# Issuing the product dt*u and the first two softmax minima one tick later

## The chip, the cores and the metric

The kernel runs on one core of a Trainium2 chip. The metric is device microseconds for one execution, as the median of several runs. A core has five engines that work side by side, each through its own queue in order: TensorE (PE, matmuls), VectorE (DVE), ScalarE (ACT), GpSimd (POOL) and SyncE (SP), which here issues all DMAs.

## The reference, cut to what matters

Two layers work on 4 images of 384 channels and 32 x 32 pixels, all in float32.

- Layer 0 is a selective scan over the 1024 pixels in four directions: groupnorm, a projection to dt, B and C, then for each of 384 channels and 16 states

```
dt = softplus(W_dt (W_x u) + bias)
h  = h * exp(dt * A) + (dt * u) * B
y  = sum over states of h * C
```

  followed by a sum over directions, a layernorm over channels, GELU and the residual.
- Layer 1 works on the 1024 pixels as tokens: layernorm, attention with one head of 384, residual; layernorm, four experts of 384 to 1536 to 384 with GELU, mixed by a top-2 gate (all four are computed densely), residual.

The reference's causal mask, softmax and gate are all computed.

## The kernel before, in words

**Units and ticks.** The scan is cut into 768 units: 4 images x 3 channel blocks of 128 x 2 pairs of directions x 2 directions x 4 groups of 4 states x 4 groups of 32 channels. A unit's tile is 128 x 1024 (32 channels x 4 states on the partitions, pixels along the row). A loop written out by hand (lines 1287 to 1315) issues one unit per turn, called a tick: `decay` puts exp(dt A) for unit t + 2 on ACT (L550), `front` the product v = du * B on DVE (L557), `back` the product h * C of unit t - 1 on POOL (L570), held until v of this tick is done, `middle` the scan on DVE (L563), and `row`, every fourth tick, the matmuls that sum over states into y (L595). While image 0 is scanned, v of many units comes from PE instead: `feed` scales a transposed du on ACT (L798, tiles st), and `turned` transposes it back on PE (L815).

**What runs between.** All other work is written as Python generators that the loop advances a little in each tick. `yield "wait", n` stops one for n ticks, `yield "pe", x` takes x us off a budget of PE work per tick (4.4 in attention, 3.3 in experts). `defer(n, f)` calls f at the beginning of the tick n later, `defer(n, f, inner)` in that tick between v and the scan. The order within a tick is: decay; deferred calls; v; the product on POOL; the `inner` calls; the scan; `row`; the fetches of dt, du, B and C for units 3 to 5 ticks ahead; one step of the next image's preparation; then side work and, with what is left of the budget, attention and experts of the image whose scan is done. So the scan of image b runs beside the preparation of image b + 1 and the attention and experts of image b - 1. After tick 768 only the last image's attention and experts are left.

**Projection (L407 to L445).** `preparation(b)` calls `project_dt` for each channel block m and pair, twelve ticks apart from b = 1 on. In tick s it takes its tiles and issues the matmuls of the first half (L423); in s + 1 softplus of that half on ACT (L429) and the matmuls of the second; in s + 2 its softplus; in s + 3 the store of dt for the first direction (L435) and the product dt*u on DVE (L437); in s + 4 the store of that du (L439), the store of dt and the product of the second direction; in s + 5 the last store. The loads of later units read dt and du back from DRAM.

**Slots.** Eight tiles of SBUF, the slots, are shared by projection, experts' weights (w, up to four chunks ahead, L1102 to L1109), layernorm's squares (three), attention's tiles, residual tiles (xe, xr) and `feed`. `take` waits for a free one; a slot given back rests one tick and goes to the end of the line. Four PSUM banks (two while image 0 is scanned) are shared in the same way.

**Attention (L843 to L995).** `scores(i)` issues the score matmuls of the 128 tokens of block i (L897, and the mask's L902), one or two PSUM banks of up to 512; `softmax(i)` takes the row's minimum on DVE (L911; scores carry a minus sign), exp with its sum on ACT (L915), and gives the banks back; one tick later the row is normalised. Block i is transposed for the value product when the scores of block i + 3 are due, one block per tick.

Of the kernel before, what the change touches and what calls it, by code (L numbers as in the profile page):

```python
# [15 lines left out]
P = 128  # L16
# [4 lines left out]
L = HW * HW  # L21
# [28 lines left out]
def hybrid_kernel(  # L50
# [63 lines left out]
    inner = {}  # L114

    def defer(ticks, f, where=due):
        where.setdefault(clock[0] + ticks, []).append(f)

    class Shared:
# [31 lines left out]
    slots = Shared(  # L151
        SLOTS, lambda i, name, *shape: slotp.tile(list(shape), F32, tag=f"s{i}", name=name), 1
    )
# [139 lines left out]
    def columns(v):  # L293

        return v.rearrange("p (h w) -> p w h", w=HW)
# [111 lines left out]
    def project_dt(b, pair, m, u, xd):  # L407

        ks = PAIRS[pair]
        while not slots.ready(3 + pair):  # L410
            yield "wait", 1
        v = u[m]
        if pair == 1:
            v = slots.now(f"ut_{b}_{m}", P, L)
            nc.scalar.copy(v.rearrange("p (w h) -> p w h", h=HW), columns(u[m]))
        dts = [slots.now(f"dt_{b}_{k}_{m}", P, L) for k in ks]
        for h in range(NH):
            while not banks.ready(2):
                yield "wait", 1
            pss = [banks.now(f"pdt_{b}_{k}_{m}_{h}") for k in ks]  # L420
            for i, k in enumerate(ks):
                r = slice(64 * pair + 32 * i, 64 * pair + 32 * i + R)
                nc.tensor.matmul(  # L423
                    pss[i], wdt[r, m * P : (m + 1) * P], xd[r, bass.ts(h, 512)],
                    start=True, stop=True,
                )
            yield "wait", 1
            for i, k in enumerate(ks):
                nc.scalar.activation(  # L429
                    dts[i][:, bass.ts(h, 512)], pss[i], AF.Softplus, bias=dtb[:, k, m : m + 1]  # L430
                )
                banks.give(f"pdt_{b}_{k}_{m}_{h}")
        yield "wait", 1
        for i, k in enumerate(ks):
            nc.sync.dma_start(dts_d[b, k][0, m * P : (m + 1) * P, :], dts[i])  # L435
            du = yield from slots.take(f"du_{b}_{k}_{m}", P, L)
            nc.vector.tensor_mul(du, dts[i], v)  # L437
            yield "wait", 1
            nc.sync.dma_start(dts_d[b, k][1, m * P : (m + 1) * P, :], du)  # L439
            if b == 0:  # L440
                stored_du.add((k, m))
            slots.give(f"dt_{b}_{k}_{m}", f"du_{b}_{k}_{m}")
        if pair == 1:
            slots.give(f"ut_{b}_{m}")
# [34 lines left out]
    def preparation(b):  # L479

        u = first_x if b == 0 else load_image(b)
        yield "wait", 3
        yield from groupnorm(b, u)
        while clock[0] < IMAGE * (b - 1) + 24:

            yield "wait", 1
        xd = one.tile([P, L], F32, tag="xd", name=f"xd_{b}")
        if b == 0:
            nc.scalar.activation(dump, eps, AF.Softplus)
            scan_weights()  # L490
        yield from project_x(b, 0, u, xd)
        if b == 0:
            fetch(-3, ("bc",))
            first_dt(u, xd)
            yield "start", 0
        yield from project_x(b, 1, u, xd)
        for m in range(M):
            for pair in range(2):
                if b > 0 or m > 0 or pair > 0:
                    yield from project_dt(b, pair, m, u, xd)  # L500
                yield "wait", 0 if b == 0 and m == 0 else 12
# [341 lines left out]
    def attention(b, yb, fx0):  # L843
# [47 lines left out]
        def scores(i):  # L891
            ss = []
            for o in range(0, (i + 1) * P, 512):
                e = min((i + 1) * P, o + 512)
                ps = yield from banks.take(f"ss_{b}_{i}_{o}")
                for c in range(M):
                    nc.tensor.matmul(  # L897
                        ps[:, : e - o], qt[:, c, i * P : (i + 1) * P], xn[:, c, o:e],
                        start=(c == 0), stop=(c == M - 1 and e <= i * P),
                    )  # L900
                if e > i * P:
                    nc.tensor.matmul(ps[:, e - o - P : e - o], ident, causal, start=False, stop=True)  # L902
                ss.append((o, e, ps[:, : e - o]))
                yield "pe", 2.6 * (e - o) / 512
            pr = prs[i] = yield from slots.take(f"pr_{b}_{i}", P, L)
            defer(1, lambda: softmax(i, ss, pr), inner)

        def softmax(i, ss, pr):
            nb = sm.tile([P, 4], F32, tag="nb", name=f"nb_{b}_{i}")
            for n, (o, e, ps) in enumerate(ss):  # L910
                nc.vector.tensor_reduce(nb[:, n : n + 1], ps, AX.X, ALU.min)  # L911
            if len(ss) == 2:
                nc.vector.tensor_tensor(nb[:, 0:1], nb[:, 0:1], nb[:, 1:2], ALU.min)
            for n, (o, e, ps) in enumerate(ss):
                nc.scalar.activation(  # L915
                    pr[:, o:e], ps, AF.Exp, bias=nb[:, 0:1], scale=-1.0,
                    accum_out=nb[:, 2 + n : 3 + n],
                )
                banks.give(f"ss_{b}_{i}_{o}")
            defer(1, lambda: normalise(i, nb, len(ss)))  # L920

        def normalise(i, nb, n):
            wd = (i + 1) * P
            if n == 2:
                nc.vector.tensor_add(nb[:, 2:3], nb[:, 2:3], nb[:, 3:4])
            nc.vector.reciprocal(nb[:, 2:3], nb[:, 2:3])
            nc.scalar.activation(prs[i][:, :wd], prs[i][:, :wd], AF.Copy, scale=nb[:, 2:3])
# [62 lines left out]
        for n in range(NB + 3):  # L990
            if n >= 3:
                yield from turn(n - 3)
            if n < NB:
                yield from scores(n)
            yield "wait", 1  # L995
            if n >= 3 and n % 2 == 0:
                yield from values((n - 3) // 2)
# [372 lines left out]
```

## Time and profile before

| | |
|---|---|
| Median of 5 runs | 3821.51 us (3819.53 to 3822.94) |
| The profiled execution | 3824.38 us |
| Its span | 3822.6 us |
| Busy in the span: PE, DVE, ACT, POOL | 89%, 78%, 55%, 48% |
| Mean granted PE clock | 0.915 |
| Scan of a unit on DVE, 768 times | 2284 ns each |
| Product v on DVE, 688 times | 1242 ns each |
| Product dt*u on DVE, 46 times | 1491 ns (ut) and 1401 ns (x) each |
| Product h * C on POOL, 768 times | 2367 ns each |

The scans begin at 47.7 us; image 0's scan lasts until some 714 us, and the last scan starts at some 3147 us. From there on the last image's attention and experts keep PE busy to the end. A row of the groups or the timeline has: source line, engine, operation, result <- inputs with their tiles' names, shape, count, busy time, mean; and in the timeline, in brackets, how long the engine stood still before it and for whom. The view of waits adds these idle times up by pairs: who waited, for whom, microseconds in total, times, the longest. The chain is followed back from the last instruction: at each step to what released it.

### The profile page before, as it was taken

How to read it: one execution, taken by the hardware profiler on the slowest of the kernel's cores; microseconds unless marked ns; L12 is line 12 of the kernel's file. 1: busy time of each engine (PE TensorE's matmuls, PEld its weight loads, DVE VectorE, ACT ScalarE, POOL GpSimd, SP SyncE). 2: the span in 40 equal slices, each digit the busy share in tenths (PEclk: the TensorE clock that was granted, in tenths of full speed). 3: DMA queues.
4: the chain of work that ended last, by engine and by line, in shares of the span. 5: the costliest groups of instructions: out<-in, count | busy, mean ns of one | idle time of the engine just before them, and what ended most of it. 6: DMA issues, size and time to landing. Idle time of an engine off the chain costs nothing.

```text
span 3822.6 us, 33900 instructions
## 1 busy us (share of the span) xinstructions
PE 3383.2 (89%) x11367; PEld 1502.9 (39%) x11367; DVE 2990.5 (78%) x2094; ACT 2104.6 (55%) x2695; POOL 1816.6 (48%) x776
## 2 busy tenths in 40 slices
PE   4666665689999999799999999789999999999999
PEld 1123332235334334345333343354343434644444
DVE  6999899998899999989988999999999992210000
ACT  4688988555666656556565555455555552422121
POOL 2677677644455555545555565455566560000000
PEclk7676677689999999999999999899999999999999
DMA  6564555445576666535756656345566551222321
GB/s 209 206 221 180 214 201 212 182 155 186 182 245 224 220 241 224 178 120 204 240 190 229 215 195 208 136 151 205 198 208 232 190 180 38 89 74 84 94 84 52
DMA packets 407838, 678.26 MB, mean 177 GB/s; under 512 B 33472, under 2 KB 280560, under 8 KB 407664
## 3 DMA queue, kind: packets, MB, share of 16 engines
q1 hardware_dynamic: 401456, 675.70, 51.6%
q8 instruction: 90, 1.47, 0.2%
q10 hardware_dynamic: 6208, 0.39, 0.1%
q14 instruction: 84, 0.69, 0.1%
HBM read 604.04 MB, written 71.96 MB: 177 GB/s over the span
## 4 chain that ended last, share of the span: by engine, by line
PE 42%; DVE 38%; ACT 10%; issue 7%; DMA 2%; POOL 1%; SPq 0%; DVEq 0%; POOLq 0%; ACTq 0%
DVE h L563 22%; PE ph L1154 15%; PE fy L1179 14%; DVE v L557 11%; PE y L595 3%; ACT da L550 3%; ACT st L798 2%; PE pq L868 2%; PE pv L879 2%; PE ss L897 2%; DVE fy L1188 1%; PE po L963 1%; PE pxd L392 1%; ACT L550 1%; ACT L429 1%
## 5 line engine op out<-in xcount | busy, mean ns | idle before, releaser
L570 POOL TENSOR_TENSOR h<-h,bc 128x1024 f32<-128x1024 f32 x768 | 1815.5, 2367 | 1334.8 <-DVE v L557 1147.1
L563 DVE TENSOR_TENSOR_SCAN h<-da,v 128x1024 f32<-128x1024 f32 x768 | 1751.5, 2284 | 109.5 <-PE v L815 18.5
L550 ACT ACTIVATE da<-dt,a 128x1024 f32<-128x1024 f32 x768 | 875.9, 1146 | 937.4 <-DVE h L563 890.3
L1154 PE MATMUL ph<-fx,w 128*128 128x512 f32 x2304 | 1022.6, 600 | 7.0 <-ACT dt L429 3.0
L1179 PE MATMUL fy<-ht,w 128*128 128x512 f32 x2304 | 1022.5, 601 | 1.0 <-ACT dt L429 0.9
L557 DVE TENSOR_TENSOR v<-du,bc 128x1024 f32<-128x1024 f32 x688 | 854.2, 1242 | 34.9 <-DMA du<-dts 14.8
L1154 PEld LDWEIGHTS ph<-fx,w 128*128 128x128 f32 x2304 | 434.4, 191 | 583.2 <-issue 531.0
L1179 PEld LDWEIGHTS fy<-ht,w 128*128 128x128 f32 x2304 | 436.9, 192 | 576.0 <-issue 551.6
L595 PE MATMUL y<-h,sel 128*32 128x512 f32 x3072 | 533.5, 676 | 140.5 <-POOL h L570 140.4
L1139 ACT ACTIVATE ht<-ph,b1s 128x512 f32<-128x512 f32 x384 | 257.5, 678 | 459.2 <-PE ph L1154 458.4
L1188 DVE SCALAR_TENSOR_TENSOR fy<-fy,b2s,tw 128x512 f32<-128x512 f32 x96 | 72.2, 752 | 426.0 <-PE fy L1179 426.0
L595 PEld LDWEIGHTS y<-h,sel 128*32 128x32 f32 x3072 | 101.4, 116 | 478.5 <-POOL h L570 248.4
L815 PE MATMUL v<-ident,st 128*128 128x128 f32 x640 | 134.2, 381 | 98.5 <-DVE h L563 96.9
L798 ACT ACTIVATE st<-dut,bt 128x128 f32<-128x128 f32 x640 | 205.0, 501 | 0.1
L1143 ACT ACTIVATE ht<-ht 128x3072 f32<-128x3072 f32 x64 | 176.8, 2763 | 0.8
L815 PEld LDWEIGHTS v<-ident,st 128*128 128x128 f32 x640 | 109.2, 199 | 161.1 <-issue 87.8
L550 ACT ACT_TABLE_LOAD x110 | 141.1, 1283 | 14.1 <-DMA dt<-dts 11.0
L423 PE MATMUL pdt<-xd,wdt 12*128 12x512 f32 x184 | 84.0, 805 | 65.6 <-ACT dt L429 34.2
L963 PE MATMUL po<-pt,vt 128*128 128x256 f32 x480 | 105.3, 368 | 7.3 <-ACT pt L859 7.3
L897 PE MATMUL ss<-axn,qt 128*128 128x512 f32 (+3 forms) x288 | 105.2, 512 | 3.1 <-ACT pr L915 2.7
L963 PEld LDWEIGHTS po<-pt,vt 128*128 128x128 f32 x480 | 93.1, 195 | 22.6 <-ACT pt L859 9.5
L911 DVE TENSOR_REDUCE nb<-ss 128x1 f32<-128x512 f32 (+3 forms) x48 | 26.0, 553 | 79.0 <-PE ss L902 63.7
(201 smaller groups left out, 1653.5 us busy)
## 6 DMA issues: line engine op xcount, KB each, us to landing
bc<-rows SPq DMA_DIRECT2D x384, 512.0 KB, 4.8
w<-in_w SPq DMA_DIRECT2D x384, 384.0 KB, 6.1
dt<-dts SPq DMA_DIRECT2D x192, 512.0 KB, 4.2
du<-dts SPq DMA_DIRECT2D x192, 512.0 KB, 6.7
dts<-dt SPq DMA_DIRECT2D x48, 512.0 KB, 3.6
dts<-du SPq DMA_DIRECT2D x48, 512.0 KB, 3.5
fx<-t2d SPq DMA_DIRECT2D x12, 768.0 KB, 6.0
tw<-mkd SPq DMA_DIRECT2D x32, 256.0 KB, 6.7
```

The lines of the kernel that those rows point to most:

```text
L550: nc.scalar.activation(u["da"], spread["dt4", n], AF.Exp, scale=a4[:, g, u["q"] : u["q"] + 1])
L557: return nc.vector.tensor_tensor(u["v"], spread["du4", n], spread["bc", n][:, 0, :], ALU.mult)
L563: nc.vector.tensor_tensor_scan(u["h"][:, ::step], u["da"][:, ::step], u["v"][:, ::step], 0.0, op0=ALU.mult, op1=ALU.add,)
L570: product = nc.gpsimd.tensor_tensor(h, h, spread["bc", n][:, 1, :], ALU.mult)
L595: nc.tensor.matmul(y, sel, h, start=first, stop=last, tile_position=(0, jj * DJ))
L798: nc.scalar.activation(st[:, t, :].rearrange("p (d i) -> p i d", i=NI)[:, i, :], dut[:, t, :], AF.Copy, scale=bt[:, u["pair"], t, u["i"] * ...
L815: nc.tensor.transpose(u["v"][:, t * P : (t + 1) * P], st[:, t, u["j"] * P : (u["j"] + 1) * P], ident)
L897: nc.tensor.matmul(ps[:, : e - o], qt[:, c, i * P : (i + 1) * P], xn[:, c, o:e], start=(c == 0), stop=(c == M - 1 and e <= i * P),)
L963: nc.tensor.matmul(pv[:, o:], vt[:, j, m * P : (m + 1) * P], pts[step][j // 4][:, j % 4, o:], start=False, stop=(j == nj - 1),)
L1139: nc.scalar.activation(ht[:, f, :], ps, AF.Identity, bias=bias)
L1154: nc.tensor.matmul(ps, tiles[n][:, c, (f % 2) * P : (f % 2 + 1) * P], xns[h][:, c, :], start=(c == 0), stop=(c == M - 1),)
L1179: nc.tensor.matmul(pss[m], tiles[n][:, f, :], hts[fh][:, f, :], start=(fh == 0 and f == 0), stop=(fh == 1 and f == FH - 1),)
```

## The change

In `project_dt` the two du tiles are taken together with the dt tiles at the start, so that 4 slots (pair 0) or 5 (pair 1) have to be free then, instead of 3 or 4. Both stores of dt are issued in tick s + 3. For images 1 to 3 there is then one tick more before the first product, so that the products come in s + 4 and s + 5, the stores of du in s + 5 and s + 6, and the slots are given back a tick later; for image 0 the products stay in s + 3 and s + 4. In attention, the softmax of blocks 0 and 1 is called two ticks after their scores instead of one; blocks 2 to 7 keep one.

```diff
     def project_dt(b, pair, m, u, xd):
 
         ks = PAIRS[pair]
-        while not slots.ready(3 + pair):
+        while not slots.ready(4 + pair):
             yield "wait", 1
...
-        dts = [slots.now(f"dt_{b}_{k}_{m}", P, L) for k in ks]
+        dts, dus = ([slots.now(f"{x}_{b}_{k}_{m}", P, L) for k in ks] for x in ("dt", "du"))
...
         yield "wait", 1
         for i, k in enumerate(ks):
             nc.sync.dma_start(dts_d[b, k][0, m * P : (m + 1) * P, :], dts[i])
-            du = yield from slots.take(f"du_{b}_{k}_{m}", P, L)
+        if b > 0:
+
+            yield "wait", 1
+        for i, k in enumerate(ks):
+            du = dus[i]
             nc.vector.tensor_mul(du, dts[i], v)
             yield "wait", 1
             nc.sync.dma_start(dts_d[b, k][1, m * P : (m + 1) * P, :], du)
...
             pr = prs[i] = yield from slots.take(f"pr_{b}_{i}", P, L)
-            defer(1, lambda: softmax(i, ss, pr), inner)
+            defer(2 if i < 2 else 1, lambda: softmax(i, ss, pr), inner)
```

## The prediction

> **What bounds the kernel now.** I read the profile in this order: the busy shares, the busy time by windows, VectorE's (DVE's) waits, the chain of waits, and then the rows around each wait that the change can touch. One tick of the schedule is one unit: a product v (1.24 us) and a scan (2.28 us) on DVE; where nothing else is in the way, scans start 3.69 us apart.
>
> ```profile
> PE 3383.2 (89%) x11367; PEld 1502.9 (39%) x11367; DVE 2990.5 (78%) x2094; ACT 2104.6 (55%) x2695; POOL 1816.6 (48%) x776
> ...
> 800.00:1000.00 200.00, 185.95 (x763) 99.86 (x764) 173.04 (x148) 122.80 (x171) 98.04 (x42) 0.95 0.49 168
> 1000.00:1600.00 600.00, 578.84 (x1821) 233.24 (x1820) 570.60 (x386) 365.20 (x352) 344.07 (x146) 0.98 0.64 220
> ...
> 1800.00:2400.00 600.00, 584.65 (x1810) 234.59 (x1808) 561.99 (x368) 347.83 (x332) 345.06 (x147) 0.98 0.62 208
> 2400.00:2600.00 200.00, 167.78 (x710) 90.90 (x711) 186.55 (x148) 93.76 (x132) 99.57 (x43) 0.91 0.46 163
> 2600.00:3148.00 548.00, 543.04 (x1679) 220.06 (x1678) 526.52 (x343) 294.69 (x283) 328.03 (x140) 0.99 0.59 201
> ...
> PE 42%; DVE 38%; ACT 10%; issue 7%; DMA 2%; POOL 1%; SPq 0%; DVEq 0%; POOLq 0%; ACTq 0%
> ```
>
> In a windows row the second number is TensorE (PE) busy, the fourth DVE, the fifth ScalarE (ACT). While experts run (1000 to 1600, 1800 to 2400, 2600 to 3148), PE is busy 96 to 99% and DVE 94 to 96%: two engines sit at the limit together, and the chain changes between them. A DVE wait there is worth no more than what PE can follow. Before 800 us there are no experts and the chain runs over DVE and ACT; after 3148 us it is PE alone. The waits in question:
>
> ```profile
> DVE nb L911 <- PE ss L902: 63.7, 16, 30.5
> ...
> DVE du L437 <- PE ph L1154: 13.0, 2, 8.7
> DVE du L437 <- PE fy L1179: 11.1, 4, 6.1
> ...
> DVE du L437 <- ACT dt L429: 7.0, 9, 2.0
> ...
> DVE du L437 <- DMA dts<-du: 1.2, 1, 1.2
> ...
> 837.06 0.29 DVE L911 TENSOR_REDUCE nb<-ss 128x1 f32<-128x128 f32 x1 [5.34 <-PE ss L902]
> ...
> 1668.08 0.29 DVE L911 TENSOR_REDUCE nb<-ss 128x1 f32<-128x128 f32 x1 [10.76 <-PE ss L902]
> ...
> 2490.74 0.29 DVE L911 TENSOR_REDUCE nb<-ss 128x1 f32<-128x128 f32 x1 [6.16 <-PE ss L902]
> ```
>
> Columns: total, times, longest; then start, duration, and in brackets the idle before. The minimum of the first score block of images 0, 1, 2 holds DVE for 5.34, 10.76 and 6.16 us; the 30.5 us is image 3's, where DVE has no scans left and the wait is free. The product dt*u loses 32.3 us in all, of which 27.9 lie in images 1 and 2 beside attention and experts. One projection while image 0 is scanned shows a second loss:
>
> ```profile
> 509.88 3.06 DVE L437 TENSOR_TENSOR du<-dt,ut 128x1024 f32<-128x1024 f32 x1 [0.53 <-ACT dt L429]
> ...
> 515.06 1.19 DVE L437 TENSOR_TENSOR du<-dt,ut 128x1024 f32<-128x1024 f32 x1
> ...
> 509.49 2.36 POOL L570 TENSOR_TENSOR h<-h,bc 128x1024 f32<-128x1024 f32 x1 [1.00 <-DVE h L563]
> ```
>
> The product came 0.53 us late for softplus; meanwhile GpSimd (POOL) started its own product, and the DVE instruction shows 3.06 us instead of 1.19. The second of the pair did not wait and took 1.19.
>
> **The change, part by part.** No operation is added or removed: 46 DVE products, 96 DMA stores and the minima keep their number and size, so all of it is position.
>
> *A. Image 1's six projections, beside image 0.* Three first products (509.88, 566.45, 624.45) lose 0.53 + 0.50 + 0.52 in waits and (3.06 + 3.04 + 3.02) - 3 x 1.20 = 5.52 in length: 7.1 us. A tick later softplus is long done, the product goes straight behind its scan, and this goes. Each projection now lasts a tick longer, so starts move from ticks 111, 128, 145, 162, 179, 196 to 111, 129, 147, 165, 183, 201 (counted from the waits in the code), and their softplus against ACT's feed copies in other ticks: two scans that waited 3.67 and 3.13 us for PE transposes stuck behind a projection matmul may be spared or another may get this (plus or minus 4). But the chain in those stretches is largely ACT (copies st, softplus, table loads), so some of the 7.1 is found waiting for ACT. I take -5; ends -11 and +2. Next late there: ACT's decays. Image 0's own five projections keep their product's tick and count nothing.
>
> By the Trainium skill (SBUF - State Buffer, section Who interferes with whom), a DVE instruction with two SBUF inputs and a GpSimd one exclude each other, and issue order decides who blocks; the 3.06 beside 1.19 agrees. The rule speaks against the change: were the moved product always second, it would lose up to one POOL product, 2.37 us, twelve times, and part A would be +28 - 7, not -5.
>
> *B. The end of image 1's projection.* The last one ends at tick 207 instead of 201 and holds five of eight slots while attention of image 0 asks for four at tick 206. Three slots have just been used by the x tiles, the third rests until 207, so by my count attention starts one tick late: +3.7 at most once. Experts of image 0 end at tick 393, attention of image 1 starts at 398 with its image, so that most of the shift is taken up there. I take +2; ends 0 and +7.4 (two ticks).
>
> *C. Softmax 0 and 1.* Each wait above can shrink by one tick, 3.69: ceiling -11.0. What is late next is PE itself. Image 0: PE next waits 1.99 us at 847.18 for POOL's h, which DVE's lead shortens, then scores 4 hold DVE: -2. Image 1: PE runs without a gap from 1624 to 1687 (value, pxd and score matmuls); softmax 1 and 2 now meet in one tick and wait for scores 2: 0. Image 2: PE waits 1.70 for h at 2497: -1.7. Their two exps, sums and bank releases move along; the turn of block 0 three ticks after its scores still finds it normalised. Sum -3.7; ends -11 and +1. Image 3 waits on PE either way.
>
> *D. dt*u of images 2 and 3.* The waits are 4.31, 1.95, 4.21, 1.18, 6.12, 0.39, 0.61, 8.71 and 0.39, 27.9 us. Those named PE come from a slot that a weight tile left a tick before and that PE still reads; taken at the projection's start, the slot is long free, and softplus has a tick more. I expect nearly all of these waits to go. DVE then leads, and PE must follow: what PE itself loses to DVE and POOL in these stretches (y waiting for h) is 2.0 + 8.5 + 5.8 = 16.3 us. Half of that, -8; ends -28 (PE follows wholly) and 0 (PE is the bound).
>
> *E. Slots and queues.* A projection asks for 4 or 5 free slots at once instead of 3 or 4 and holds them to its end. Experts keep four weight tiles ahead; with five slots out, three are left. A chunk is 5.15 us of PE and a weight DMA lands 6.1 us after issue, so two chunks (10.3) still cover it; beside a residual tile or layernorm's squares (one and three slots) a projection starts late or experts miss a tick. SyncE's queue (SP) carries it: the second store of dt moves a tick earlier, both stores of du a tick later, past fetches of later units; they are due hundreds of us later, while the weight loads behind them wait on the same softplus as now (151.9 us over 22 waits, 6.9 each). POOL's queue gets nothing. I take one lost tick in one of the eleven projections beside experts: +3.5; ends 0 and 11 x 3.69 = +40.6.
>
> Sum: -5 + 2 - 3.7 - 8 + 3.5 = -11.2. The profiled execution took 3824.38 us (span 3822.6), 2.9 over the median of the runs; 3824.38 - 11.2 = 3813.2, and on the median 3821.51 - 11.2 = 3810.3.
>
> **The rivals.** *R1, DVE alone is the bound*: all waits turn into time. For it: scans 3.69 us apart over long stretches with no wait on PE. Against: PE 96 to 99% busy there. With -7.1 in A, -11 in C, -27.9 in D and +2 + 3.5 it is -40.5 at the most; PE's limit halves D and C: about -24, 3797. *R2, PE takes it all*: C and D are worth 0, since PE was late and stays late; A + B = -3, 3818.5. For it: the chain at 1624 to 1687 and at 2063 to 2077 goes by PE, across the longest waits. Against: PE's own 16.3 us. *R3, slower, by the slots*: experts run dry of slots during projections and lose a tick of PE in each. It costs 3.69 per projection; at all eleven 40.6, so 3821.5 - 14.7 + 40.6 = 3847; it decides against the change from the fourth lost tick on, and past 0.2% from the seventh (14.7 + 7.6 = 22.3). For it: eight slots, a residual tile out for 12 to 14 ticks of every 64. Against: PE now waits for weights 2.8 us in all. *R4, the tick changes nothing*, because the callback runs in the same place: excluded by the schedule's dictionary, in which the entry for tick t + 2 is read one turn later.
>
> **How the numbers follow.** 0.2% of 3821.5 is 7.6 us, about what a measurement of this kernel can tell from no change: faster is below 3813.9, slower above 3829.1. Chances: the forecast 0.45 (its own range 3803 to 3817, 0.09 of it above 3813.9), R1 0.14, R2 0.22 (0.02 of it below 3813.9), R3 0.19 (from 3829 to 3847). Faster: 0.36 + 0.14 + 0.02 = 0.52; same: 0.09 + 0.20 = 0.29; slower: 0.19. The range runs from 3796 (leaves out half of R1) to 3833 (leaves out most of R3).
>
> **What would show it.** A: no product dt*u over 1.4 us in the first 700 us beyond image 0's own three. B: the first q matmul, now at 800.8, at about 799. C: waits of nb at the three places of about 1.7, 7 and 2.5 us, and at 1674 a new one for softmax 2. D: no du wait on ph or fy left; if PE's busy share between 1800 and 2400 rises above 97.5%, PE followed; if new waits at fy or at nb hold as much, R2. E: PE waits for weights well over 2.8 us, or expert matmuls missing a tick, mean R3. Wrong would be the forecast if ACT, not DVE, set the pace of image 0 in all six projections, or if attention's start slipped in every image.

## The result, and the profile after

| | runs | median | against before |
|---|---|---|---|
| before | 44 | 3821.67 us (3816.68 to 3826.85) | |
| after | 26 | 3825.86 us (3820.19 to 3830.49) | 1.0011 (95%: 1.0006 to 1.0017) |

The change costs about 4 us, within the 0.2% that the prediction calls no change, though the interval lies above 1; a gain of 11 us had been forecast. The result lies in the forecast's range, on the other side of before. Below, ratios are turned into microseconds with 3821.5 (0.1% is 3.8). The ratio of an experiment is against runs of before taken beside it, whose medians lay between 3818.8 and 3821.4 us; so ratios are compared, and not the times.

The profiled execution of after has a span of 3822.0 us, 0.6 less than that of before, while the medians say 4.2 more. Two executions of one kernel lie up to 10 us apart, so a pair of profiles is read here stretch by stretch, never by its total.

The busy shares and some windows of the kernel after, as shown of before (in a windows row: start and end, length, PE, PE's weight loads, DVE, ACT, POOL busy):

```profile
PE 3376.0 (88%) x11367; PEld 1499.6 (39%) x11367; DVE 2988.8 (78%) x2094; ACT 2103.8 (55%) x2694; POOL 1819.1 (48%) x776
...
800.00:1000.00 200.00, 177.21 (x742) 96.16 (x742) 169.41 (x144) 117.10 (x166) 95.12 (x41) 0.94 0.43 150
1000.00:1600.00 600.00, 585.60 (x1841) 236.10 (x1840) 564.29 (x381) 357.28 (x347) 342.01 (x145) 0.99 0.65 223
1800.00:2400.00 600.00, 588.18 (x1854) 238.34 (x1855) 567.78 (x372) 358.53 (x345) 346.82 (x147) 0.99 0.62 215
...
2600.00:3148.00 548.00, 540.36 (x1677) 219.48 (x1676) 526.23 (x342) 297.73 (x285) 329.23 (x140) 1.00 0.61 201
```

A window holds somewhat other units in the two kernels, so these rows are only a first hint. Beside the experts PE is busier in two windows of three (1000 to 1600: 578.84 before, 585.60 now; 1800 to 2400: 584.65 and 588.18, which is 98.0%; 2600 to 3148: 543.04 and 540.36). PE falls most in the first window, from 185.95 to 177.21; DVE falls there from 173.04 to 169.41, and from 1000 to 1600 us from 570.60 to 564.29. The waits of the kernel after (total, times, longest):

```profile
DVE nb L915 <- PE ss L906: 50.8, 12, 31.2
...
DVE rs_ff L687 <- ACT rs_ff L682: 27.1, 4, 12.0
...
DVE fx L703 <- PE rb_ff L693: 14.8, 3, 6.2
...
PE ph L1158 <- DMA w<-in_w: 14.2, 4, 8.5
...
DVE du L441 <- ACT dt L429: 11.9, 7, 3.8
```

No product dt*u waits for PE's ph or fy any more (before: 24.1 us). In exchange layernorm's rows wait longer (rs_ff 18.9 before, fx 8.5), the products wait longer for softplus (7.0), and PE waits 14.2 us for weights (2.8). Single instructions of after, from its timeline:

```profile
514.48 1.43 DVE L441 TENSOR_TENSOR du<-dt,ut 128x1024 f32<-128x1024 f32 x1
...
838.76 0.28 DVE L915 TENSOR_REDUCE nb<-ss 128x1 f32<-128x128 f32 x1
...
1674.38 0.29 DVE L915 TENSOR_REDUCE nb<-ss 128x1 f32<-128x128 f32 x1 [6.80 <-PE ss L906]
...
2488.38 0.29 DVE L915 TENSOR_REDUCE nb<-ss 128x1 f32<-128x128 f32 x1 [1.66 <-PE ss L906]
```

The three products of image 1 that took 3.02 to 3.06 us now take 1.43 (514.48), 1.20 (at 577.58) and 1.35 (at 637.87), and the minima wait 0, 6.80 and 1.66 us instead of 5.34, 10.76 and 6.16. So the waits that the change was aimed at are gone or shorter; only the product's wait for softplus has grown, and in image 1 two later minima now wait 2.24 and 1.47 us. Where the time went is seen by comparing when the scan of the same unit starts. From the scans of the traces, start minus that in the kernel before, us (negative is earlier; e7 to e12 are experiments below; differences of up to 2.7 us are found at unit 100 already, before anything has changed):

```
unit    after     e7     e9     e8    e11    e10    e12     e4
 208     -7.4   -4.1   -6.0   -8.2   -8.5   -2.2   -0.5   +2.7
 248    -11.9   -2.5   -8.9   -7.4  -13.9  -12.1   -5.0   -5.4
 256     +1.9   +8.4   -8.9   -6.8   -6.7  -11.5   -5.0   -2.3
 288     +1.4  +13.1   -8.9   -3.9   -7.5   -5.4   -5.0   +0.1
 384     +7.1  +10.5   -7.7  -11.5   -1.4   -2.4   +1.5   +5.2
 464    +14.6   +7.3  -10.0   -6.7   +5.5   +0.7   -0.7   +9.2
 512     -2.7   +8.0   -9.6  -24.0  -11.8  -17.4   -1.5   -8.0
 608     +0.6   +6.8   -9.7  -17.7   -7.8  -16.9   -4.2   -1.6
 767     -1.3   +6.1   -9.9  -21.5  -10.5  -20.5   -5.7   -3.8
```

After is 12 us ahead at unit 248 and 2 behind at unit 256. This is what its timeline shows just before:

```profile
939.47 4.44 PE L1158 MATMUL ph<-fx,w 128*128 128x512 f32 x6 [8.51 <-DMA w<-in_w]
...
943.95 0.69 ACT L1143 ACTIVATE ht<-ph,b1s 128x512 f32<-128x512 f32 x1 [10.64 <-PE ph L1158]
...
944.78 0.17 DVE L1031 TENSOR_REDUCE red<-sc 128x4 f32<-128x16 f32 x1 [5.67 <-ACT sc L1029]
...
945.70 2.84 PE L392 MATMUL pxd<-x,wx 128*128 128x512 f32 x6
...
979.96 0.95 DVE L687 RECIPROCAL rs_ff<-rs_ff 128x128 f32<-128x128 f32 x1 [5.27 <-ACT rs_ff L682]
...
995.65 1.75 DVE L703 TENSOR_TENSOR fx<-fx,rb_ff 128x1536 f32<-128x1536 f32 x1 [6.24 <-PE rb_ff L693]
```

PE stands still 8.51 us for the first expert weights of image 0. ACT, whose next instruction copies that matmul's result, stands 10.64 us with the decays and the gate's exp queued behind it, and DVE waits 5.67 us for that exp. The x projection of image 2 (pxd) comes after all this. In the kernel before, it lies ahead of the first expert matmul, which then finds its weights there:

```profile
939.54 4.52 PE L392 MATMUL pxd<-x,wx 128*128 128x512 f32 x6
943.89 5.31 PE L1154 MATMUL ph<-fx,w 128*128 128x512 f32 x12
```

The gate costs DVE two waits there as well, 2.91 us for its matmul and 2.34 us for its exp. So the scan of after does not fall behind at once: it loses 12.5 us from unit 248 to 251, at the two waits of layernorm, 5.27 and 6.24 us. The chain leads back from there, through PE's and ACT's work without a long gap, to the transfer of the weights (7.97 us on the chain, from 931.46). Why the x projection is later is counted from the code's waits: image 2's preparation begins after image 1's last projection. Six projections of a tick more each put it six ticks later, the x projection at tick 241 instead of 235, the first products at 252 and 253 instead of 245 and 247.

### The profile page after: what moved, and what is told of

It is laid out like the page before. It is cut to its first block, busy times and chain, and to the rows that moved or that the text cites. A ratio compares the mean times of both kernels' runs of the same rounds, so it can differ in the third digit from the quotient of the medians.

```text
span 3822.0 us, 33876 instructions
## 1 busy us (share of the span) xinstructions
PE 3376.0 (88%) x11367; PEld 1499.6 (39%) x11367; DVE 2988.8 (78%) x2094; ACT 2103.8 (55%) x2694; POOL 1819.1 (48%) x776
## 3 DMA queue, kind: packets, MB, share of 16 engines
q8 instruction: 90, 1.47, 0.2%
## 4 chain that ended last, share of the span: by engine, by line
PE 42%; DVE 33%; ACT 7%; issue 5%; DMA 3%; POOL 1%; SPq 0%; DVEq 0%; POOLq 0%; ACTq 0%
DVE h L567 20%; PE ph L1158 15%; PE fy L1183 14%; DVE v L561 9%; PE y L599 3%; ACT da L554 2%; PE pq L872 2%; PE pv L883 2%; DMA du<-dts 1%; PE ss L901 1%; PE po L967 1%; DMA w<-in_w 1%; ACT ht L1147 1%; DVE fy L1192 1%; PE v L819 1%
## 5 line engine op out<-in xcount | busy, mean ns | idle before, releaser
L1158 PE MATMUL ph<-fx,w 128*128 128x512 f32 x2304 | 1035.6, 605 | 30.2 <-DMA w<-in_w 14.2
L599 PE MATMUL y<-h,sel 128*32 128x512 f32 x3072 | 520.2, 673 | 118.6 <-POOL h L574 118.2
L554 ACT ACT_TABLE_LOAD x108 | 138.6, 1283 | 14.5 <-DMA dt<-dts 11.1
```

The source lines that it names most:

```text
L554: nc.scalar.activation(u["da"], spread["dt4", n], AF.Exp, scale=a4[:, g, u["q"] : u["q"] + 1])
L599: nc.tensor.matmul(y, sel, h, start=first, stop=last, tile_position=(0, jj * DJ))
L1158: nc.tensor.matmul(ps, tiles[n][:, c, (f % 2) * P : (f % 2 + 1) * P], xns[h][:, c, :], start=(c == 0), stop=(c == M - 1),)
```

## The experiments

The first four set the slots (theory S, step E and rival R3 of the prediction) against the rest of the change, part by part.

### e1: the projection's part alone

```diff
-            defer(2 if i < 2 else 1, lambda: softmax(i, ss, pr), inner)
+            defer(1, lambda: softmax(i, ss, pr), inner)
```

(against the kernel after)

> The project_dt part of the change alone; softmax 0 and 1 stay one tick behind their scores. Theory S (the early slots starve experts and give back what the later product saves): within 6 us of before, and like the changed kernel, with PE waiting over 10 us for weights. Rival P (the projection part saves, and the moved softmax costs): 5 us or more below before.

3830.32 us, 1.0026 (1.0016 to 1.0035): 10 us slower than before, which neither theory had. All of the loss is in the projection's part. PE waits 12.1 us for weights, over 10 as theory S had it, but 8.28 of it is for the first expert weights, as in after.

### e2: the softmax part alone

```diff
-            defer(1, lambda: softmax(i, ss, pr), inner)
+            defer(2 if i < 2 else 1, lambda: softmax(i, ss, pr), inner)
```

(against the kernel before)

> The softmax part alone; project_dt as before. S: 0 to 4 us below before, the first minima of images 0 to 2 wait about 1.7, 7 and 2.5 us instead of 5.3, 10.8 and 6.2. P: slower than before by 4 us or more, since softmax 1 and 2 now meet in one tick.

3818.2 us, 0.9993 (0.9984 to 1.0002): -2.7 us, between -6.1 and +0.8. Between after and e1, which differ by the same edit, it is 0.0015, 5.7 us. Its scans gain 2.5, 2 and 3.2 us at the attention of images 0, 1 and 2.

### e4: the slots and stores alone

```diff
-        if b > 0:
-
-            yield "wait", 1
         for i, k in enumerate(ks):
             du = dus[i]
```

(against the kernel after, with e1's edit)

> The du slots are taken at the start of the projection and both dt stored in one tick, but the product stays in its tick; softmax as before. S: slower than before by 4 to 12 us, PE waits for weights over 10 us, and the three products of about 3.05 us stay. P: at or below before, since the waits for slots that PE still reads (24 us) are gone.

3818.47 us, 0.9994 (0.9985 to 1.0004). In all, the early slots cost nothing that can be seen; PE waits 5.8 us for weights, not over 10, and theory S falls. The products now wait 13.7 us for softplus, before 7.0. The last column of the table shows that they do something: 17.2 us gained between units 464 and 512, most of it lost again around it.

### e6: early slots and the added tick for image 1 alone, its starts kept

```diff
-                yield "wait", 0 if b == 0 and m == 0 else 12
+                yield "wait", 0 if b == 0 and m == 0 else 11 if b == 1 else 12
```

(against the kernel before, with the change's edits of `project_dt` for b == 1 alone)

> Early slots and the later product for image 1 alone (its projections lie beside image 0's scan, before any experts), with eleven ticks instead of twelve between them, so that every other tick of the schedule is that of before. S: 4 to 8 us below before; unit 192 begins 4 to 8 us earlier and this lead reaches the end. Rival: the lead is there at unit 192 and is gone at the last unit, total within 3 us of before.

3818.92 us, 0.9997 (0.9988 to 1.0005). The long products are gone here (1.20 to 1.49 us for all of image 1), and little is gained: at unit 208 the scan is 0.8 us ahead. Counted from unit 110, which leaves out the differences from before the change, the scans up to unit 208 take 356.7 us before, 354.1 in e6 and 349.2 in after. Most of what makes after 7.4 us early at that unit is therefore not the product's later place.

That left the ticks themselves. Theory T says that the starts of image 1's projections, a tick further apart each, gain time in image 0, and that the six ticks by which they push image 2's preparation lose more. The next four vary only waits of `preparation`.

### e7 and e9: the kernel before with other waits, and nothing else

e7:

```diff
-                yield "wait", 0 if b == 0 and m == 0 else 12
+                yield "wait", 0 if b == 0 and m == 0 else 13 if b == 1 else 12
```

> The kernel before, with 13 instead of 12 ticks between the projections of image 1 and nothing else: no product is issued later after its softplus, no slot is taken earlier. The starts go to those of the changed kernel (111, 129, 147, ...) and image 2's preparation starts six ticks later, so that its x projection comes at tick 241 instead of 235. Theory T (what moves the time is where the ticks fall, not the product or the slots): image 0's scan runs ahead by 4 to 7 us at unit 208, 9 to 14 us are lost between units 248 and 256, where the x projection no longer fills the time in which PE waits for the first expert weights, and the whole takes +2 to +8 us against the kernel before; PE waits for in_w 8 us or more at once near 930 us. Rival (it is the product's place and the slots that cost): within 3 us of before, no wait on in_w over 3 us.

e9, which gives the six ticks back after the last projection:

```diff
-                yield "wait", 0 if b == 0 and m == 0 else 12
+                yield "wait", 0 if b == 0 and m == 0 else 12 if b != 1 else 7 if m == M - 1 and pair == 1 else 13
```

> The kernel before with 13 instead of 12 ticks between the projections of image 1, and 7 after the last of them, so that everything from image 2's preparation on lies at the ticks of before. Theory T: the 4 to 7 us that image 0's scan runs ahead at unit 208 are kept to the end or lost only in part: -3 to -7 us against before. Rival (image 0's lead is caught by something later, PE for one): within 2 us of before.

e7: 3829.91 us, 1.0024 (1.0014 to 1.0034). e9: 3811.83 us, 0.998 (0.9971 to 0.9988). Both follow theory T, each a little beyond its range (9.2 us slower where up to 8 was expected, 7.6 faster where up to 7 was). The product, the slots and the softmax are those of before in both, yet one is 9 us slower and the other 8 us faster, and they differ only in when image 2's preparation starts. That start alone is worth 0.0044, 17 us. DVE's waits between 900 and 1030 us, first of e7, then of e9:

```profile
DVE red L1027 <- ACT sc L1025: 9.3, 1, 9.3
DVE rs_ff L683 <- ACT rs_ff L678: 6.5, 1, 6.5
DVE fx L699 <- PE rb_ff L689: 4.9, 1, 4.9
```

```profile
DVE du L437 <- PE ph L1154: 4.3, 1, 4.3
DVE fx L651 <- PE mu_ff L638: 3.2, 1, 3.2
DVE sc L1012 <- PE pgate L1005: 2.9, 1, 2.9
DVE red L1027 <- ACT sc L1025: 0.7, 1, 0.7
```

The three waits of e7 are those of after; e9 has the wait for the gate's exp at 0.7 instead of 9.3 and none for rs_ff or rb_ff.

### e8: the changed kernel, image 2's preparation at the tick of before

```diff
-                yield "wait", 0 if b == 0 and m == 0 else 12
+                yield "wait", 0 if b == 0 and m == 0 else 6 if b == 1 and m == M - 1 and pair == 1 else 12
```

> The changed kernel, with 6 instead of 12 ticks of rest after image 1's last projection, so that image 2's preparation starts at the tick that it has in the kernel before (its x projection at 235, its first products at 246 and 247). The slots and the later products stay as changed. Theory T: the loss of 9 to 14 us between units 248 and 256 goes, PE waits for in_w about 3 us in all, and the kernel takes -4 to -9 us against before (3812 to 3818). Rival (the slots or the later product cost, wherever the preparation starts): +2 to +6 us against before, as the changed kernel.

3802.55 us, 0.9955 (0.9942 to 0.9967): 17 us faster than before, 21 faster than after, by one constant. It is more than theory T had. The same place in its timeline:

```profile
930.20 2.74 PE L392 MATMUL pxd<-x,wx 128*128 128x512 f32 x6
...
941.82 4.32 PE L1158 MATMUL ph<-fx,w 128*128 128x512 f32 x6
...
946.17 0.69 ACT L1143 ACTIVATE ht<-ph,b1s 128x512 f32<-128x512 f32 x1 [3.20 <-PE ph L1158]
...
947.00 0.17 DVE L1031 TENSOR_REDUCE red<-sc 128x4 f32<-128x16 f32 x1 [0.85 <-ACT sc L1029]
```

PE has the x projection to do (its second half at 936.46) while the weights land; the copy waits 3.20 us instead of 10.64 and the gate's exp holds DVE 0.85 instead of 5.67. That alone is no gain, since the gate's matmul now stands behind the x projection and DVE waits 5.41 us for it. The gain comes after it: from 900 to 1030 us DVE's waits are 13.1 us in all here, and 21.6 in after.

### e10: the changed kernel, all projections at or beside the starts of before

```diff
-                yield "wait", 0 if b == 0 and m == 0 else 12
+                yield "wait", 0 if b == 0 and m == 0 else 11 if b > 0 else 12
```

> The changed kernel with 11 instead of 12 ticks between the projections of images 1, 2 and 3, which takes the added tick back in the rest after each, so that projections start at or beside the ticks of before. The products, the slots and the softmax stay as changed. Theory T: no lead at unit 208 (0 to -2 us, as the starts of image 1 are those of before), no loss at units 248 to 256, the minima give -2 to -4: -2 to -8 us against before in all. Rival (the slots or the later product cost beside the experts): +2 us or more.

3802.8 us, 0.9952 (0.9939 to 0.9964): 18 us faster. It has no lead at unit 208 to speak of (-2.2), as expected, but twice the expected gain in all, made beside the experts.

The last three ask what made up the 21 us between e8 and after, what in e10 gains, and whether the two gains add.

### e11: x projection early, products late

```diff
         yield from project_x(b, 1, u, xd)
+        if b == 2:
+            yield "wait", 6
         for m in range(M):
```

(against e8)

> The changed kernel with image 2's preparation started at the tick of before (x projection at tick 235), and six ticks of rest put behind that x projection, so that all twelve products of image 2 lie at the ticks of the changed kernel (252, 253, 271, ...). It splits the shift of the preparation in two. If the loss is the x projection that no longer covers PE's wait for the first expert weights, it goes wholly: 3801 to 3806, as with the preparation's start kept. If it is where the six projections fall against experts and layernorm, nothing is gained: 3822 to 3828. Half and half, as the scan's lead says (about 9 us between the two at unit 256, 20 at the end): 3810 to 3816, without a wait for in_w over 4 us near 930 us.

3814.86 us, 0.9989 (0.998 to 0.9997). Half and half, as the scan's lead had it: 0.0022 (8 us) lie between after and e11, where only the x projection's place differs, and 0.0034 (13 us) between e11 and e8, where only the six projections' place does. PE does not wait for the first expert weights in e11, as expected. The second part is lost between units 288 and 348 (11 us by the scans), 7.3 of it in two stalls that after has too. One of them, in the timeline of after:

```profile
1149.13 1.27 ACT L429 ACTIVATE dt<-pdt,dtb 128x512 f32<-128x512 f32 x2
...
1152.88 1.28 ACT L1147 ACT_TABLE_LOAD   x1
...
1154.17 2.76 ACT L1147 ACTIVATE ht<-ht 128x3072 f32<-128x3072 f32 x1
...
1158.83 1.27 ACT L429 ACTIVATE dt<-pdt,dtb 128x512 f32<-128x512 f32 x2
1159.55 1.22 DVE L441 TENSOR_TENSOR du<-dt,x 128x1024 f32<-128x1024 f32 x1 [3.80 <-ACT dt L429]
```

The two halves of softplus should lie one tick (3.69 us) apart. The expert's GELU (2.76 us, with table loads of 1.28 before and after it) comes between them, they are 9.70 us apart, and the product, though a tick later than before, still waits 3.80 us. In e8 DVE has no wait at all for any other engine between 1145 and 1540 us; in e11 it has 13.8 us there, 7.3 of them for softplus.

### e12: e10 with the slot of du taken when the product is issued

```diff
-        while not slots.ready(4 + pair):
+        while not slots.ready(3 + pair):
...
-        dts, dus = ([slots.now(f"{x}_{b}_{k}_{m}", P, L) for k in ks] for x in ("dt", "du"))
+        dts = [slots.now(f"dt_{b}_{k}_{m}", P, L) for k in ks]
...
-            du = dus[i]
+            du = yield from slots.take(f"du_{b}_{k}_{m}", P, L)
```

(against e10)

> The changed kernel with 11 instead of 12 ticks between the projections of images 1, 2 and 3, and with the slot of du taken when its product is issued, as before; the added tick and the softmax stay. The products of image 2 then lie at the ticks of before (245, 247, 263, 265, ...). If the early slot is what frees PE and VectorE beside the experts, the 13 us that the same kernel with early slots gains between units 416 and 512 go, the products wait for PE's ph and fy again (20 us or more in all), and the time is -3 to -8 us against before (3813 to 3818). If the tick alone does it: 3800 to 3805.

3819.82 us, 0.9998 (0.999 to 1.0007). The gain is gone, all of it, and the waits are back:

```profile
DVE du L441 <- PE fy L1183: 23.4, 5, 7.1
...
DVE du L441 <- PE ph L1158: 4.3, 1, 4.3
```

In e10 the product waits for softplus alone, 3.4 us in all. So the gain beside the experts needs the early slots, which I had put down as the change's price: 0.0046, 17.6 us between e10 and e12. A tick more without them gives nothing there. But the slots alone don't give it either: e4, which has them with the product in its old tick, gains 2.3 us, and its products wait 13.7 us for softplus. Softmax, worth about 3 to 6 us, does not close the 16 us between e4 and e10. It takes both, the slots against the weight tiles and the tick against softplus. The time of e12 is somewhat above the expected 3813 to 3818.

A part of the gain between units 464 and 512 is work put off. In every kernel with early slots beside the experts the last projection of image 3 gets its five slots late: the copy of ut, which follows this wait in the code, comes at unit 518 in after and at 500 in before. In after its first product comes at unit 521 (2147.81 us), 29 units after that of the projection before it (2030.73), where 18 were due; in e10 and e4 it is at 520 and 519, 32 units after, where 17 were due. In before it is at 502, 17 after, and in e12 at 504. How much of the 17 us is this was not measured apart.

### e13: both at once

```diff
-                yield "wait", 0 if b == 0 and m == 0 else 12
+                yield "wait", 0 if b == 0 and m == 0 else 11 if b > 1 else 6 if b == 1 and m == M - 1 and pair == 1 else 12
```

(against the kernel after)

> The changed kernel with image 1's projections at its new starts (13 ticks between), image 2's preparation started at the tick of before, and 11 ticks between the projections of images 2 and 3. If the lead of image 1's new starts (9.5 us where it was measured alone) adds to what the kernel with all starts kept gains (18.5): 3791 to 3797. If the two meet the same limit, TensorE beside the experts: 3799 to 3804, no faster than either alone.

3805.31 us, 0.9969 (0.9959 to 0.998): 12 us faster than before, not faster than e8 or e10. It has image 0's lead (-9.5 at unit 208) but ends at -18.9, where e10, without that lead, ends at -20.5. The two gains don't add; the expected equal of the better one, 3799 to 3804, was missed by one microsecond. Which later wait takes the lead back was not settled.

## Why the prediction was wrong, step by step

The five terms of the forecast add up to -11.2. What they left out is worth +21, and it turned the sign.

- **A (-5; scan 7.4 us ahead at unit 208).** The size is near, but by luck: the reason is wrong. The three long products went as forecast, and in e6 this is worth 2.6 us by the scans and 1 us by the time (-4.6 to +1.9). Other waits take their place: DVE's waits in that stretch are 23.6 us before and 25.4 in e6, with 2.8 for GpSimd instead of 0.3 and 2.5 for PE's y instead of none. Most of the lead comes from the new starts 129, 147, 165, ..., which I had listed as a side effect of plus or minus 4; e9 has them without any of the change and gains 7.6 us to the end. The worst case that I had set against the change with the Trainium skill's rule (SBUF - State Buffer, Who interferes with whom) would have made A +21; no product of image 1 took more than 1.43 us.
- **B (+2): the step that failed.** "Experts of image 0 end at tick 393, attention of image 1 starts at 398 with its image, so that most of the shift is taken up there." I followed the shift of image 1's last projection to the attention, where it does cost the one tick that I had counted (softmax 0 is called at tick 220 instead of 218, one of the two by its own edit; the first q matmul comes at 801.15 us, not at 799). I did not follow it to the next item of the same generator, image 2's preparation, which starts six ticks later for the whole of image 1's scan. That moved the x projection off the place where PE waits for the first expert weights, and moved the projections onto layernorm and GELU. By e8 against after it costs 21 us (8 for the x projection, 13 for the six projections); by e9 against e7, without any of the change, 17.
- **C (-3.7).** Right: -2.7 (-6.1 to +0.8) in e2, 5.7 between e1 and after. The three waits came to 0, 6.80 and 1.66 us where about 1.7, 7 and 2.5 had been named, with the new wait for scores 2 behind the second (2.24).
- **D (-8).** Right in kind. The waits on weight tiles went, and PE's busy share between 1800 and 2400 passed the 97.5% that was named. Part of the gain was taken back: of some 17 us that the scans of after, e8, e10 and e4 gain between units 464 and 512 alike, 5 to 9 are returned by unit 592, where the projection that was put off has to be done; what PE's own limit has in this was not measured. The size stays open: by e10 against e12 slots and tick together are worth 17.6 us, twice the forecast.
- **E (+3.5, up to +40.6).** The loss was not found, though the sentence "a projection starts late" came true once, for image 3's last, by 11 ticks in after and 15 in e10 and e4; no run shows what that costs. PE does wait 14.2 us for weights, which the prediction had named as the sign of rival R3, but 8.5 of it is the first weight tile with the x projection moved away; with the same slots and the start kept it is 3.7 (e8) and 3.2 us (e10). The sign was right for a loss and wrong for its cause.

With B's missing part taken out, the forecast of 3810 stands against 3802.6 for e8 and 3802.8 for e10, inside the whole range (3796 to 3833) and just below the forecast's own (3803 to 3817). How e8's -17.2 is made up is not settled: -7.6 (starts of image 1) and -2.7 (softmax) would leave -7 for the rest, but e13 shows that the starts don't add to the other gains. Rival R1's price was also summed wrongly: with C and D halved it is -7.1 - 5.5 - 14 + 5.5 = -21, some 3800 us, not -24 and 3797.

e8 and e10 are faster than before by about 0.45%, and than after by 0.55 to 0.6%; each is the change with one constant of the rest between projections adjusted.

## What to carry to other kernels

Where work is laid out by ticks, an edit that makes a step one tick longer moves everything that follows it in the same generator: write down the new tick of every later item, down to the next image, and ask what each had been covering. A wait for a transfer is covered by the work that stands ahead of it in its engine's queue (here the x projection: no wait with it, 8.51 us without); see what that work is before it is moved. And judge such a change with the later starts held fixed as well, since otherwise it is measured together with a new phase, which here was worth +21 and -8 us.

## What the runs showed that I had not expected

- One copy on ACT that waited for a matmul held everything behind it: 10.64 us in after, 13.11 in e7, and DVE, which only needed the gate's exp from behind it, for 5.67 and 9.31 us.
- A tick more between six projections gains 7.6 us when the next preparation keeps its start (e9) and loses 9.2 when it moves with them (e7): the rest between steps alone moves this kernel as far as the edit's own effects do.
- A change of function on ACT costs 1.28 us here and next to nothing beside it: in after the softplus that starts at 1149.13 ends at 1150.40, the table load runs from 1150.42 to 1151.70, and the next decay starts at 1151.71. The Trainium skill (ScalarE: Activation LUTs, What ACT_TABLE_LOAD costs) gives 1283 ns for the load, as here, and about 1380 ns for a drain with it, 2.66 us in all; this drain is not seen at that place.
